# Fourteen picked tiles for twelve, and another order of the stages, in two layers of a graph attention kernel

## The chip, the cores and the metric

The kernel runs on one NeuronCore of a Trainium2 chip. The time is that of one launch on the device, in microseconds. TensorE (PE), VectorE (DVE), ScalarE (ACT) and GpSimd (POOL) each run their own list of instructions in order and wait for one another by semaphores; SyncE (SP) issues most DMAs.

## The reference

A graph with 6250 nodes of 64 features and 206250 directed edges, sorted by destination, goes through three layers of attention over the edges. Cut to what is computed:

```python
for i in range(3):
    q, k, v = (x @ W[i] + b[i] for W, b in ((Wq, bq), (Wk, bk), (Wv, bv)))
    e = edge_attr @ We[i]
    alpha = sum(q[dst] * (k[src] + e), -1) / sqrt(64)
    p = exp(alpha - segment_max(alpha, dst)[dst])
    w = p / segment_sum(p, dst)[dst]
    x = segment_sum((v[src] + e) * w[:, None], dst) + x @ Ws[i] + bs[i]
    x = relu(x)                  # and a layer norm after layers 0 and 1
out = layernorm(x_in + log_softmax(x))
```

## The kernel before

The edges are cut into tiles of 128. Six tiles make a chunk, four chunks a unit; there are 67 full units and one of four tiles. The destinations of a chunk lie within 32 nodes, so the four chunks of a unit share the 128 partitions of a score matrix, 32 each. The keys and values are not made for each edge: the weights are folded into the query, and an edge brings only the 64 features of its source node and its own 64 attributes. In layer 0 the kernel also sorts each unit's edges, so that in layers 1 and 2 the source nodes of a tile's two halves fall into known windows of 1024 nodes each. The change is about layers 1 and 2.

There are two ways to bring the source rows of a tile. POOL *gathers* it: one indirect DMA from the node table in DRAM (`gather`, L607; a small copy on ACT, the gate of L639, releases it). Or TensorE *picks* it: the table also lies in SBUF as two summands (`parts`), VectorE writes a one-hot matrix by comparing the tile's keys with a ramp (`hot`, L1342), and eight matmuls of 128x256 (L1404) serve one tile position of a pair of chunks, two tiles; VectorE then takes the right quarter of the result with a copy (L1365) and three predicated copies (L1367), called the evacuation, and ACT swaps some halves (L1353 to L1355). `PICKS` says how many of a unit's 24 tiles are picked, `depth` spreads them over the two pairs of chunks: 12 are (3, 3) positions. `Picker.picks` makes of this picks of one or two positions, here four a unit: of 16, 8, 16 and 8 matmuls. `Picker.aim` issues the `hot` instructions; at a unit's end it does so for the whole next unit. Four `hot` buffers and two banks of `ps_x` serve them.

The main loop goes over units; unit u has four quarters j, one for each chunk, and in the same pass it works on older and newer units:

- `turn(j)` (L1705, L1708): three transposes of chunk j's source rows into a bank `ps_a`, and two copies on ACT into `featT`, or `fourth` for the last chunk. The edges' half of it comes from DRAM by SP (`across`, L1685).
- `products(u-1, h)`, h = 0, 1 (L1718): half of the scores, into `ps_s` and `ps_p`; `most(u-1, h)` (L1732, L1745): mask and running maximum on VectorE; `powers(u-1)` (L1751): the exponential on ACT; `weights(u-1, h)` (L1765, L1768): the transposes of the exponentials through `ps_s` and `ps_p`, copied by ACT to `probT`.
- `sums(u-2)` (L1777): 48 matmuls in the profile, which add up the rows weighted by `probT` in `ps_p`; ACT copies them to `part`, SP stores that. `refill(u-2)` then gives the unit's buffer to unit u+2, and `free(u, j)` releases gathers for that unit.
- one pick for unit u+1 in each quarter, and one step of `finish` in quarter 0: every 5 to 6 units a group of four 128-node blocks is normalised (L1532, L1554) and, in layers 0 and 1, projected for the next layer (L1449, L1454, L1463).

Nothing reorders this: the instructions stand on each engine as the Python code issues them. A stage of an older unit is put between those of the present one so that no engine waits for another.

Of the kernel before, what the change touches and what calls it, by code (L numbers as in the profile page):

```python
# [19 lines left out]
P = 128  # L20
# [25 lines left out]
HALF = NW // 2  # L46
GC = 16
ROWS = 8
PICKS = ((8,), (12,), (12,))
LEAD = (3, 1, 1)  # L50
NH = WB // KB

# [377 lines left out]
def main_path(  # L430
# [1175 lines left out]
    class Unit:  # L1606
# [160 lines left out]
                self.probT = work.tile([P, TC, P], F32, name="probT", bufs=1)  # L1767
            nc.scalar.copy(self.probT[:, t0 : t0 + m, :n], p_t[:, :, :n])  # L1768

        def sums(self):  # L1770

            p_g = ps("g")[:, :P]
            batch = loaded[self.layer, self.k]
            for t in range(self.tiles):
                for j in range(self.m):
                    rows = slice(j * W, (j + 1) * W)
                    nc.tensor.matmul(  # L1777
                        p_g[rows, :].rearrange("n (h d) -> n h d", h=2),
                        self.probT[:, t, rows],
                        batch[:, j, t],  # L1780
                        start=(t == 0),
                        stop=(t == self.tiles - 1),
                    )
            nc.scalar.copy(self.part[: self.rows, :P], p_g[: self.rows, :])

        def store(self, half=None):
            for j in range(self.m):
# [81 lines left out]
    class Line:  # L1869


        def __init__(self, layer):
            self.layer = layer
            self.todo = list(zip(done, groups))
            self.stored = self.summed = 0
            self.halved = -1

        def sums(self, u):
            if u < 0:
                return  # L1880
            chunks[self.layer, u].sums()
            self.summed = u + 1

        def refill(self, u):
            if u >= 0:
# [54 lines left out]
    for layer in range(L):  # L1940
        line = Line(layer)
        assert not picked(layer, 0)

        def free(u, j):
            lead = 2 * LB if not layer else min(2 * LB, LB + u)
            release(layer, u * LB + j + (0 if not layer else 1) + lead, nc.scalar.copy)

        picker = Picker(layer)
        for u in range(NU - 2):
            this = chunks[layer, u]  # L1950
            picking = picker.batch(u + 1)
            n = len(picker.picks(u + 1))
            pace = 0 if layer else 6 if u < 3 else 3
            while not opened:
                move(1)
            line.sums(u - 2)
            line.products(u - 1, 0)
            if waiting:
                active.append(waiting.pop(0))
            for j in range(LB):  # L1960
                picker.quarter = j
                if j == 2 and not layer:
                    line.weights(u - 1, 0)
                this.turn(j)
                if j == 0:
                    line.refill(u - 2)
                free(u, j)
                if j == 0 and layer:
                    line.most(u - 1, 0)
                if j == 1 and layer:  # L1970
                    line.products(u - 1, 1)
                if j == 2 and layer:
                    line.powers(u - 1)
                if j == 3 and layer:
                    line.weights(u - 1, 1)
                if j == 1:
                    line.begun()
                    if not layer and placed(0, u + 1):
                        line.most(u - 1, 1)
                        line.powers(u - 1)  # L1980
                a, b = -(-n * j // LB), -(-n * (j + 1) // LB)
                if layer:
                    for i in range(max(b - a, 1)):
                        next(picking, None)
                        if not i and j == 1:
                            line.most(u - 1, 1)
                if j == 0:
                    close_up()
                else:
                    step()  # L1990
                if not layer:
                    move(pace - pace // 2)
                    if j == 0:
                        line.most(u - 1, 0)
                    for _ in range(b - a):
                        next(picking, None)
                    move(pace // 2)
                    picker.evacuate()
                if j == 0:
                    if not layer:  # L2000
                        line.products(u - 1, 1)
                        if not placed(0, u + 1):
                            line.most(u - 1, 1)
                            line.powers(u - 1)
                    ask(layer, u + 1)
                    if not placed(layer, u + 1):
                        chunks[layer, u + 1].across()
                if j == 2:
                    line.weights(u - 1, 0 if layer else 1)
                    if not this.placed:  # L2010
                        this.uncode()
                    decode(layer, u + 2)
                    if placed(layer, u + 1):
                        chunks[layer, u + 1].across()
                        chunks[layer, u + 1].shade()
                if j == 3:
                    line.store()
            assert next(picking, None) is None
            if any(not pair for _, pair, *_ in picker.swaps):
                picker.flush()  # L2020
            picker.ready.update(keys)
            picker.aim()
            for k in range(u + 2, u + 4):
                decode(layer, k)

        picker.flush()
        more = layer + 1 < L
        for _ in sorting:
            pass
        serve()  # L2030
        assert not picker.todo and not picker.hots
        if more:
            current[0] = layer
            lacking.extend(range(NW))
            if not layer:
                early.close()
                psum.append(ctx.enter_context(tc.tile_pool(name="psum", bufs=1, space=bass.MemoryType.PSUM)))
                bank_of.update({"g": "p", "node": "a", "s1": "p", "w0": "s"})
                stock[0] = ctx.enter_context(tc.tile_pool(name="picks", bufs=2))
                parts.append(stock[0].tile([P, 2, HALF * WB, D], F32R, name="parts", bufs=1))  # L2040
        u = NU - 2
        full = chunks[layer, u]
        line.sums(u - 2)
        line.refill(u - 2)
        line.scores(u - 1, 0)
        full.turn(0)
        free(u, 0)
        line.scores(u - 1, 1)
        ask(layer, u + 1)
        last = chunks[layer, u + 1]  # L2050
        last.across()
        last.shade()
        close_up()
        full.turn(1)
        free(u, 1)
        line.store()
        line.weights(u - 1, 0)
        close_up()
        full.turn(2)
        free(u, 2)  # L2060
        line.weights(u - 1, 1)
        full.turn(3)
        free(u, 3)
        free(u, 4)
        assert not pending
        close_up()
        line.scores(u, 0)
        line.scores(u, 1)
        line.sums(u - 1)
        line.refill(u - 1)  # L2070
        line.store()
        close_up()
        last.turn(0)
        last.uncode()
        line.weights(u, 0)
        line.weights(u, 1)
        close_up()
        line.scores(u + 1, 0)
        line.scores(u + 1, 1)
        line.sums(u)  # L2080
        line.refill(u)
        line.store()
        close_up()
        line.weights(u + 1, 0)
        line.weights(u + 1, 1)
        close_up()
        line.sums(u + 1)
        line.refill(u + 1)
        line.store()
        close_up()  # L2090
        if more:
            decode(layer + 1, 0)
            decode(layer + 1, 1)
            decode(layer + 1, 2)
            ask(layer + 1, 0)
            chunks[layer + 1, 0].across()
            chunks[layer + 1, 0].shade()
        while active or len(ending) > 1:
            close_up()
        while ending and (not more or (layer, groups[-1][0]) not in written):  # L2100
            close_up()
        if more:
            assert all((layer, g) in written for g, n in groups)
            for k in range(FB):
                if (layer + 1, k) not in loaded:
                    fetch(layer + 1, k)
                if k:
                    await_turn(layer + 1, k)
                else:
                    gather_all(layer + 1, k)  # L2110
            while lacking or held:
                reload(layer + 1)
            while ending:
                close_up()
# [45 lines left out]
```

## Time and profile before

| | |
|---|---|
| median of 3 runs | 4164.22 us (4156.0 to 4164.31) |
| profiled execution: time, span of its profile | 4160.32 us, 4158.5 us |
| TensorE's mean granted clock | 0.925 |
| PE, PEld (weight loads) busy | 3390.2 us (82%), 2406.9 us (58%) |
| DVE, ACT, POOL busy | 3094.5 us (74%), 2344.7 us (56%), 2819.2 us (68%) |
| gathers on POOL in layers 1 and 2 (L607) | 1592 of 985 ns |

A group's line names line, engine, operation, result and operands; then the count, the busy time in us, the mean ns of one, the idle time ahead of it and what ended that. In a timeline a row has start and length in us, and in brackets the idle time ahead of it with its releaser. A run of matmuls is pipelined, so the next run may start before it ends. Layer 0 takes the first 1900 us or so of the span, layers 1 and 2 some 1100 each.

### The profile page before, as it was taken

How to read it: one execution, taken by the hardware profiler on the slowest of the kernel's cores; microseconds unless marked ns; L12 is line 12 of the kernel's file. 1: busy time of each engine (PE TensorE's matmuls, PEld its weight loads, DVE VectorE, ACT ScalarE, POOL GpSimd, SP SyncE). 2: the span in 40 equal slices, each digit the busy share in tenths (PEclk: the TensorE clock that was granted, in tenths of full speed). 3: DMA queues.
4: the chain of work that ended last, by engine and by line, in shares of the span. 5: the costliest groups of instructions: out<-in, count | busy, mean ns of one | idle time of the engine just before them, and what ended most of it. 6: DMA issues, size and time to landing. Idle time of an engine off the chain costs nothing.

```text
span 4158.5 us, 105258 instructions
## 1 busy us (share of the span) xinstructions
PE 3390.2 (82%) x34183; PEld 2406.9 (58%) x34183; DVE 3094.5 (74%) x10306; ACT 2344.7 (56%) x5994; POOL 2819.2 (68%) x2774
## 2 busy tenths in 40 slices
PE   3779988998999899995778788888758788787776
PEld 2345555555555555553666666666646666666664
DVE  5678888888888888874566677677646767777775
ACT  1345555555565565563555556665535666666665
POOL 5466666666666666663777777777747777777774
PEclk9889999999999999996899999999969999999997
DMA  5657676667667767675677777777657677777774
GB/s 120 165 163 194 175 186 177 168 181 185 174 176 186 181 174 187 171 199 137 151 181 185 189 191 188 185 190 197 167 129 183 176 185 186 185 185 190 185 185 100
DMA packets 787997, 728.88 MB, mean 175 GB/s; under 512 B 487336, under 2 KB 612450, under 8 KB 787440
## 3 DMA queue, kind: packets, MB, share of 16 engines
q1 hardware_dynamic: 630436, 504.14, 47.5%
q0 software_dynamic: 88448, 90.75, 11.8%
q10 hardware_dynamic: 68556, 127.16, 8.6%
q8 instruction: 278, 4.55, 0.5%
q14 instruction: 279, 2.29, 0.2%
HBM read 562.78 MB, written 158.81 MB: 174 GB/s over the span
## 4 chain that ended last, share of the span: by engine, by line


## 5 line engine op out<-in xcount | busy, mean ns | idle before, releaser
L607 POOL DMA_INDIRECT feat<-x,gate x1592 | 1568.8, 985 | 485.3 <-issue 367.3
L607 POOL DMA_INDIRECT feat<-in_x,gate x1100 | 1177.7, 1071 | 676.0 <-ACT gate L639 360.8
L1404 PE MATMUL ps_x<-parts,hot 128*128 128x256 f32 x6336 | 942.5, 301 | 0.0
L1404 PEld LDWEIGHTS ps_x<-parts,hot 128*128 128x128 f32 x6336 | 842.2, 202 | 82.2 <-DVE feat L1367 65.6
L1708 ACT COPY featT<-ps_a 64x384 f32<-64x384 f32 x1320 | 626.7, 475 | 410.3 <-PE ps_a L1705 392.7
L1367 DVE COPY_PREDICATED feat<-which,ps_x 128x256 f32<-128x256 int32 (+1 forms) x1584 | 592.8, 374 | 54.3
L1365 DVE COPY feat<-ps_x 128x256 f32<-128x256 f32 (+1 forms) x528 | 187.8, 356 | 580.8 <-PE ps_x L1404 564.9
L1705 PE MATMUL ps_a<-ident,feat 128*128 128x128 f32 x2380 | 450.2, 290 | 145.2 <-DMA feat<-x,gate 107.0
L1705 PEld LDWEIGHTS ps_a<-ident,feat 128*128 128x128 f32 x2380 | 285.1, 145 | 354.1 <-issue 261.1
L1081 DVE TENSOR_SCALAR hit<-ruler,pos 128x384 bf16<-128x384 f16 x1608 | 457.3, 326 | 7.3 <-PE ps_m L1101 6.6
L1342 DVE TENSOR_SCALAR hot<-keys,rank 128x512 fp32r<-128x512 f16 (+1 forms) x1040 | 432.7, 483 | 5.4 <-DMA keys<-keyS 5.4
L1777 PE MATMUL ps_p<-feat,probT 128*32 128x128 f32 x6600 | 242.8, 300 | 84.6 <-ACT probT L1768 73.8
L1092 PE MATMUL ps_x<-hit,raw 128*64 128x384 bf16 x1608 | 296.0, 364 | 0.5 <-DVE hit L1081 0.4
L1092 PE MATMUL ps_x<-hit,rest 128*64 128x384 bf16 x1608 | 277.8, 342 | 0.0
L1092 PE MATMUL ps_x<-hit,end 128*64 128x384 bf16 x1608 | 277.3, 341 | 0.0
L1777 PEld LDWEIGHTS ps_p<-feat,probT 128*32 128x32 f32 x6600 | 198.9, 122 | 123.2 <-ACT probT L1768 98.2
L1718 PE MATMUL ps_s<-featT,q 128*32 128x384 f32 x1866 | 235.2, 509 | 32.6 <-DVE most L1732 25.4
L1765 PE MATMUL ps_s<-ident,prob 128*128 128x128 f32 (+1 forms) x417 | 83.4, 313 | 215.4 <-ACT prob L1751 214.3
L1751 ACT ACTIVATE prob<-prob,part 128x768 f32<-128x768 f32 x204 | 190.0, 932 | 83.8 <-DVE part L1745 75.5
L1125 ACT COPY eT<-ps_x 128x384 f32<-128x384 f32 x268 | 129.3, 483 | 122.5 <-PE ps_x L1092 89.6
L1765 PEld LDWEIGHTS ps_s<-ident,prob 128*128 128x128 f32 (+1 forms) x417 | 47.8, 152 | 245.9 <-ACT prob L1751 241.5
L1143 ACT COPY feat<-ps_a 128x384 f32<-128x384 f32 x256 | 122.1, 481 | 120.6 <-PE ps_a L1135 89.7
(280 smaller groups left out, 6019.1 us busy)
## 6 DMA issues: line engine op xcount, KB each, us to landing
featT<-eaS SPq DMA_DIRECT2D x658, 192.0 KB
feat<-eaP SPq DMA_DIRECT2D x134, 768.0 KB
raw<-in_ea SPq DMA_DIRECT2D x536, 96.0 KB
eaS<-eT ACTq DMA_DIRECT2D x134, 384.0 KB
keys<-keyS SPq DMA_DIRECT2D x132, 384.0 KB
eaP<-feat ACTq DMA_DIRECT2D x128, 384.0 KB
shade<-maskS SPq DMA_DIRECT2D x198, 192.0 KB
fourth<-eaS SPq DMA_DIRECT2D x134, 192.0 KB
```

The costliest lines, as they stand in the source:

```text
L607: nc.gpsimd.indirect_dma_start(out=feat[:, c, t, 0], out_offset=None, in_=xts[layer][:, :], in_offset=bass.IndirectOffsetOnAxis(ap=index[: ...
L1081: nc.vector.tensor_scalar(hit, ruler, self.pos[:, at : at + 1], None, ALU.is_equal)
L1092: nc.tensor.matmul(self.px[j * D : (j + 1) * D, :HE], self.parts[2 * h + i].thirds[part][:, j, t * D : (t + 1) * D], self.hits[h, 2 * i + ...
L1342: nc.vector.tensor_scalar(hot[:, h], keys[self.layer, k][:, first : first + n], rank[:, h : h + 1], None, ALU.is_equal)
L1365: nc.vector.tensor_copy(found, px[:, :, :, 0])
L1367: nc.vector.copy_predicated(found, which[:, :, :, b].bitcast(I32).unsqueeze(3).to_broadcast([P, 2, m, D]), px[:, :, :, b],)
L1404: nc.tensor.matmul(px[:, t - t0, v].rearrange("p b d -> p (b d)"), hot[:, h, (2 * pair + v) * P : (2 * pair + v + 1) * P], those[:, i, b0 ...
L1705: nc.tensor.transpose(pt[:, t * P : (t + 1) * P], rows[:, 2 * t * D : 2 * (t + 1) * D], ident)
L1708: nc.scalar.copy(featT[:, :, h, :], pt[h * D : (h + 1) * D, : n * P].rearrange("d (i e) -> d i e", e=P))
L1718: nc.tensor.matmul(p_s[rows, :w], self.q[:, rows], self.featT[j][:, cols], start=True, stop=True)
L1751: nc.scalar.activation(self.prob[:n, : self.cols], self.prob[:n, : self.cols], AF.Exp, bias=neg, accum_out=self.part[:n, P + 1 : P + 2],)
L1777: nc.tensor.matmul(p_g[rows, :].rearrange("n (h d) -> n h d", h=2), self.probT[:, t, rows], batch[:, j, t], start=(t == 0), stop=(t == sel ...
```

## The change

`PICKS` goes from 12 to 14 in layers 1 and 2. `depth` gives (4, 3) positions, so the four picks are of 16, 16, 16 and 8 matmuls, all four `hot` buffers are in use (the fourth half as wide), and ten tiles are gathered instead of twelve. And the quarters of layers 1 and 2 get a new order: weights of unit u-2 in quarter 0, its sums in 1, both products and the first maximum of u-1 in 2 around the pick, the second maximum and the exponential in 3 ahead of the pick. The weights of a unit thus come one pass later than before. The core of the diff:

```diff
-PICKS = ((8,), (12,), (12,))
+PICKS = ((8,), (14,), (14,))
...
             while not opened:
                 move(1)
-            line.sums(u - 2)
-            line.products(u - 1, 0)
+            if not layer:
+                line.sums(u - 2)
+                line.products(u - 1, 0)
...
                 this.turn(j)
-                if j == 0:
-                    line.refill(u - 2)
-                free(u, j)
-                if j == 0 and layer:
-                    line.most(u - 1, 0)
-                if j == 1 and layer:
-                    line.products(u - 1, 1)
-                if j == 2 and layer:
-                    line.powers(u - 1)
-                if j == 3 and layer:
-                    line.weights(u - 1, 1)
-                if j == 1:
-                    line.begun()
-                    if not layer and placed(0, u + 1):
+                if layer:
+                    if j == 2:
+                        line.products(u - 1, 0)
+                        line.most(u - 1, 0)
+                        line.begun()
+                    if j == 3:
                         line.most(u - 1, 1)
                         line.powers(u - 1)
+                        free(u, j)
+                else:
...
                 if layer:
-                    for i in range(max(b - a, 1)):
+                    for _ in range(max(b - a, 1)):
                         next(picking, None)
-                        if not i and j == 1:
-                            line.most(u - 1, 1)
+                    if j == 0:
+                        line.weights(u - 2, 0)
+                        line.weights(u - 2, 1)
+                    if j == 1:
+                        line.sums(u - 2)
+                        line.refill(u - 2)
+                        free(u, j)
+                    if j == 2:
+                        line.products(u - 1, 1)
+                        free(u, j)
...
-                if j == 2:
-                    line.weights(u - 1, 0 if layer else 1)
+                if j == 2 and not layer:
+                    line.weights(u - 1, 1)
...
                 if j == 3:
                     line.store()
+                    if layer:
+                        decode(layer, u + 2)
+                        chunks[layer, u + 1].across()
+                        chunks[layer, u + 1].shade()
...
         full = chunks[layer, u]
+        if layer:
+            line.weights(u - 2, 0)
+            line.weights(u - 2, 1)
```

The `else` branch keeps the old order for layer 0. `sums` can now be issued in parts, but each call still issues all of it.

TensorE in the middle of layer 1, before, from the first weights of a unit to the first pick of the next; `hot_` and a number is one `hot` tile, and an instruction of fp32 that the profile counts twice stands here once:

```order
L1765 MATMUL ps_s<-ident,prob 128x128 x3
L1705 MATMUL ps_a<-ident,feat 128x128 x3
L1765 MATMUL ps_p<-ident,prob 128x128 x3
L1404 MATMUL ps_x<-parts,hot_38625 128x256 x8
L1777 MATMUL ps_p<-feat,probT 32x128 x24
L1718 MATMUL ps_s<-featT,q 32x384 x3
L1718 MATMUL ps_s<-fourth,q 32x384
L1705 MATMUL ps_a<-ident,feat 128x128 x3
L1404 MATMUL ps_x<-parts,hot_38852 128x256 x8
L1404 MATMUL ps_x<-parts,hot_38855 128x256 x8
```

The same engine after, from the last transposes of a unit to the sums in the next:

```order
L1705 MATMUL ps_a<-ident,feat 128x128 x3
L1404 MATMUL ps_x<-parts,hot_38837 128x256 x8
L1705 MATMUL ps_a<-ident,feat 128x128 x3
L1404 MATMUL ps_x<-parts,hot_39073 128x256 x8
L1404 MATMUL ps_x<-parts,hot_39076 128x256 x8
L1765 MATMUL ps_s<-ident,prob 128x128 x3
L1765 MATMUL ps_p<-ident,prob 128x128 x3
L1705 MATMUL ps_a<-ident,feat 128x128 x3
L1404 MATMUL ps_x<-parts,hot_39079 128x256 x8
L1404 MATMUL ps_x<-parts,hot_39082 128x256 x8
L1779 MATMUL ps_p<-feat,probT 32x128 x24
```

Between a unit's last pick and the first of the next stood the sums, a product and a transpose; now only the transpose does, and the weights and sums stand behind the first and the second pick.

VectorE before, from the second maximum of a unit to its last evacuation and the `hot` tiles of the next unit:

```order
L1732 ISA prob,most<-ps_p,shade,most 128x384
L1732 ISA most 128x1
L1745 TENSOR_SCALAR part<-most 128x1
L1365 COPY feat<-ps_x 128x2x128
L1367 COPY_PREDICATED feat<-which,ps_x 128x2x128 x3
L1365 COPY feat<-ps_x 128x2x64
L1367 COPY_PREDICATED feat<-which,ps_x 128x2x64 x3
L1331 TENSOR_TENSOR which<-kbs,four 128x64
L1342 TENSOR_SCALAR hot_39795<-keys,rank 128x512 x2
L1342 TENSOR_SCALAR hot_39798<-keys,rank 128x512 x2
L1342 TENSOR_SCALAR hot_39801<-keys,rank 128x512 x2
```

VectorE after, the same stretch:

```order
L1365 COPY feat<-ps_x 128x2x128
L1367 COPY_PREDICATED feat<-which,ps_x 128x2x128 x3
L1732 ISA prob,most<-ps_p,shade,most 128x384
L1732 ISA most 128x1
L1745 TENSOR_SCALAR part<-most 128x1
L1365 COPY feat<-ps_x 128x2x64
L1367 COPY_PREDICATED feat<-which,ps_x 128x2x64 x3
L1331 TENSOR_TENSOR which<-kbs,four 128x64
L1342 TENSOR_SCALAR hot_40052<-keys,rank 128x512 x2
L1342 TENSOR_SCALAR hot_40055<-keys,rank 128x512 x2
L1342 TENSOR_SCALAR hot_40058<-keys,rank 128x512 x2
L1342 TENSOR_SCALAR hot_40061<-keys,rank 128x256 x2
```

The second maximum now stands between the evacuations of picks 2 and 3, and the `hot` tiles still follow the last evacuation, with a fourth one of half the width.

More of the change, by code (lines that the diff above doesn't have):

```diff
@@ L1768, in weights, with sums @@
             nc.scalar.copy(self.probT[:, t0 : t0 + m, :n], p_t[:, :, :n])
-        def sums(self):
-            p_g = ps("g")[:, :P]
+        def sums(self, first, upto):
+            if not first:
+                self.summed = ps("g")[:, :P]
+            p_g = self.summed
             batch = loaded[self.layer, self.k]
-            for t in range(self.tiles):
+            for t in range(first, upto):
                 for j in range(self.m):
@@ L1783, in sums @@
                     )
-            nc.scalar.copy(self.part[: self.rows, :P], p_g[: self.rows, :])
+            if upto == self.tiles:
+                nc.scalar.copy(self.part[: self.rows, :P], p_g[: self.rows, :])
         def store(self, half=None):
@@ L1874, in __init__, with sums @@
             self.todo = list(zip(done, groups))
-            self.stored = self.summed = 0
+            self.stored = self.summed = self.tile = 0
             self.halved = -1
-        def sums(self, u):
-            if u < 0:
+        def sums(self, u, upto=TC):
+            if u < self.summed:
                 return
-            chunks[self.layer, u].sums()
-            self.summed = u + 1
+            this = chunks[self.layer, u]
+            upto = min(upto, this.tiles)
+            if upto > self.tile:
+                this.sums(self.tile, upto)
+                self.tile = upto
+            if upto == this.tiles:
+                self.summed = u + 1
+                self.tile = 0
         def refill(self, u):
@@ L1964, in main_path @@
                 this.turn(j)
-                if j == 0:
-                    line.refill(u - 2)
-                free(u, j)
-                if j == 0 and layer:
-                    line.most(u - 1, 0)
-                if j == 1 and layer:
-                    line.products(u - 1, 1)
-                if j == 2 and layer:
-                    line.powers(u - 1)
-                if j == 3 and layer:
-                    line.weights(u - 1, 1)
-                if j == 1:
-                    line.begun()
-                    if not layer and placed(0, u + 1):
+                if layer:
[4 more added lines that the diff above has]
+                    if j == 3:
                         line.most(u - 1, 1)
                         line.powers(u - 1)
+                        free(u, j)
[4 more added lines that the diff above has]
+                    if j == 1:
+                        line.begun()
+                        if placed(0, u + 1):
+                            line.most(u - 1, 1)
+                            line.powers(u - 1)
                 a, b = -(-n * j // LB), -(-n * (j + 1) // LB)
                 if layer:
-                    for i in range(max(b - a, 1)):
+                    for _ in range(max(b - a, 1)):
                         next(picking, None)
-                        if not i and j == 1:
-                            line.most(u - 1, 1)
+                    if j == 0:
+                        line.weights(u - 2, 0)
+                        line.weights(u - 2, 1)
+                    if j == 1:
+                        line.sums(u - 2)
+                        line.refill(u - 2)
+                        free(u, j)
+                    if j == 2:
+                        line.products(u - 1, 1)
+                        free(u, j)
                 if j == 0:
```

## The prediction

> **What bounds the kernel now.** I read the windows of the two layers first, then the groups of instructions in layer 1, then the timelines of GpSimd, TensorE and VectorE in single units.
>
> The windows, one for the middle of layer 1 and one for that of layer 2. After the length stand the busy microseconds (and instructions) of PE, PEld, DVE, ACT and POOL, then the granted clock, the DMA share and GB/s:
>
> ```profile
> 2100.00:3000.00 900.00, 729.33 (x7776) 596.58 (x7773) 635.78 (x1956) 538.40 (x1390) 687.82 (x697) 0.96 0.74 186
> 3150.00:4050.00 900.00, 721.96 (x7642) 607.25 (x7643) 632.30 (x1975) 554.01 (x1406) 686.95 (x700) 0.92 0.73 185
> ```
>
> PE has the most busy time, but POOL sets the pace. The group of its gathers in layer 1, and two places of its timeline:
>
> ```profile
> L607 POOL DMA_INDIRECT feat<-x,gate x697 | 688.8, 988 | 212.5 <-issue 160.7 <-DMA feat<-x,gate 15.9 <-DVE hot L1342 7.9
> ...
> 2511.44 0.94 POOL L607 DMA_INDIRECT feat<-x,gate  x1 [0.30 <-issue]
> ...
> 2515.18 1.25 POOL L607 DMA_INDIRECT feat<-x,gate  x1 [0.30 <-DMA feat<-x,gate]
> ```
>
> 688.8 busy and 212.5 idle make 901: the idle time is only the 0.30 ahead of every gather, so POOL issues gathers without a pause. A gather costs 0.94 + 0.30 = 1.24 us, and about 0.3 more beside VectorE's `hot` instructions. A unit has twelve. Layer 1 thus takes 12 x 900/697 = 15.49 us a unit, layer 2 12 x 900/700 = 15.43. The others wait for POOL, as TensorE does at 2632.20 (1.43 us for a gather) in one undisturbed unit:
>
> ```profile
> 2626.16 2.14 PE L1404 MATMUL ps_x<-parts,hot 128*128 128x256 f32 x16
> 2628.14 0.49 PE L1705 MATMUL ps_a<-ident,feat 128*128 128x128 f32 x3
> 2628.56 0.52 PE L1718 MATMUL ps_p<-featT,q 128*32 128x384 f32 x3
> ...
> 2629.34 1.21 PE L1404 MATMUL ps_x<-parts,hot 128*128 128x256 f32 x8
> 2630.39 0.38 PE L1705 MATMUL ps_a<-ident,feat 128*128 128x128 f32 x2
> 2632.20 0.33 PE L1705 MATMUL ps_a<-ident,feat 128*128 128x128 f32 x1 [1.43 <-DMA feat<-x,gate]
> 2632.30 2.12 PE L1404 MATMUL ps_x<-parts,hot 128*128 128x256 f32 x16
> 2634.61 0.55 PE L1765 MATMUL ps_s<-ident,prob 128*128 128x128 f32 x3 [0.18 <-ACT prob L1751]
> 2634.99 0.49 PE L1705 MATMUL ps_a<-ident,feat 128*128 128x128 f32 x3
> 2635.32 0.49 PE L1765 MATMUL ps_p<-ident,prob 128*128 128x128 f32 x3
> 2635.56 1.20 PE L1404 MATMUL ps_x<-parts,hot 128*128 128x256 f32 x8
> 2637.81 1.52 PE L1777 MATMUL ps_p<-feat,probT 128*32 128x128 f32 x48 [1.05 <-ACT probT L1768]
> 2639.14 0.50 PE L1718 MATMUL ps_s<-featT,q 128*32 128x384 f32 x3
> ...
> 2639.90 0.55 PE L1705 MATMUL ps_a<-ident,feat 128*128 128x128 f32 x3
> 2640.20 2.13 PE L1404 MATMUL ps_x<-parts,hot 128*128 128x256 f32 x16
> ```
>
> **The change part by part.** *Two gathers fewer.* POOL needs 10 x 1.24 us and some 0.28 more for three gathers beside the longer `hot` run: 13.2 us. It no longer sets the pace if anything else needs more. The gathers are also released later (the refill now stands behind the sums of quarter 1), but they are those of unit u+2, more than a unit ahead of their use: no cost.
>
> *Eight matmuls more.* The second pick of a unit grows from 8 to 16. A run of 16 holds TensorE for 1.98 us (2626.16 to 2628.14), one of 8 for 1.05 (2629.34 to 2630.39): +0.93 us.
>
> *The new order.* What can bind now is a ring through two engines. VectorE builds the one-hot tiles of the next unit only behind the last evacuation of this one, as before; but TensorE then had the sums, a product and a transpose (2637.81 to 2640.20) between pick 3 and the next pick 0. Now it has one transpose. So the ring is: pick 0, both weights, transpose, pick 1, sums, transpose, first product, pick 2, and from there VectorE: evacuation of pick 2, second maximum, evacuation of pick 3, `which`, first `hot`, then pick 0. VectorE's rows:
>
> ```profile
> 2618.64 0.61 DVE L1732 CUSTOM_DVE_ANT_0 prob<-ps_p,shade,most 128x384 f32<-128x384 f32 x1
> ...
> 2619.36 0.41 DVE L1365 COPY feat<-ps_x 128x256 f32<-128x256 f32 x1
> 2619.81 1.41 DVE L1367 COPY_PREDICATED feat<-which,ps_x 128x256 f32<-128x256 int32 x3
> 2622.76 0.29 DVE L1365 COPY feat<-ps_x 128x128 f32<-128x128 f32 x1 [1.53 <-PE ps_x L1404]
> ...
> 2623.96 0.22 DVE L1331 TENSOR_TENSOR which<-kbs,four 128x64 f32<-128x64 uint8 x1
> 2624.09 2.46 DVE L1342 TENSOR_SCALAR hot<-keys,rank 128x512 fp32r<-128x512 f16 x6
> ...
> 2634.46 0.42 DVE L1365 COPY feat<-ps_x 128x256 f32<-128x256 f32 x1 [1.87 <-PE ps_x L1404]
> ```
>
> TensorE's part, from start to start: pick 0 1.98; weights, weights, transpose 1.00 (by the steps 0.38, 0.33 and 0.30 at 2634.61, 2634.99 and 2639.90); pick 1 1.98; sums 1.33; transpose 0.42; product 0.78 (2628.56 to 2629.34); pick 2 to its evacuation 2.16 (2632.30 to 2634.46): 9.65 us. VectorE's part: 1.76 (1.86 less the 0.10 by which a waiting instruction starts early, as between 2622.76 and 2624.09), 0.72, 1.20, 0.13, and a third of 2.46, 0.82: 4.63. With 0.05 to hand over, the ring is **14.33 us**. The chain is serial; I allow 0.2 either way.
>
> What lies beside it at no cost: the evacuations of picks 0 and 1 and the first maximum run on VectorE while TensorE is at work, with some 1.5 us to spare; the transposes' copies, the gate copies and the swaps on ScalarE have over a microsecond each. Two waits of TensorE go: the one for the exponential (0.18 in this unit; the weights now come a quarter later) and the 1.05 us for `probT` (now covered by transpose and pick 1, 2.28 us). On SP the loads of `featT` and `shade` move from quarter 2 to 3 and stand there behind the second product and the second maximum; queued behind them are the next `q` loads and the refill, all needed a unit later: no cost; if that cover went, ScalarE's first copy of the next unit would wait, at most for those loads.
>
> Other work on TensorE in the ring: the node groups that are finished meanwhile, in the same 900 us of layer 1:
>
> ```profile
> L1454 PE MATMUL ps_a<-xT,eq 64*128 64x512 f32 x19 | 10.8, 644 | 0.0
> L1554 PE MATMUL ps_a<-ve,wT 128*128 128x64 f32 x80 | 10.5, 274 | 0.0
> L1463 PE MATMUL ps_a<-ws,xT 64*128 64x65 f32 x72 | 9.9, 278 | 0.0
> L1532 PE MATMUL ps_a<-ident,w 128*128 128x128 f32 x40 | 6.2, 278 | 0.0
> L1449 PE MATMUL ps_a<-ident,y 128*64 128x128 f32 x40 | 6.0, 272 | 0.0
> ```
>
> 43.4 us in 58.1 units is 0.75 us each; of every run some 0.16 overlaps the next one (1.21 against 1.05 above), so about **0.61**. Layer 2 has L1532 and L1554 alone: 16.7 us, by the same steps **0.23**.
>
> *The clock.* In the ring TensorE ends its last transpose at 7.49 + 1.98 + 0.76 + 0.30 + 1.05 + 0.49 = 12.07 us after pick 0 and then has nothing until 14.33: a stretch of **2.26 us** in each unit. The granted clock changes on a grid of 3.41 us. Two neighbouring pairs of such windows:
>
> ```profile
> 3956.60:3960.01 3.41, 1.57 (x14) 1.38 (x13) 3.16 (x10) 1.81 (x5) 2.50 (x4) 1.00 0.93 204
> 3960.01:3963.42 3.41, 3.41 (x33) 3.11 (x35) 0.74 (x3) 2.35 (x6) 2.80 (x3) 0.50 0.83 218
> ...
> 2058.79:2062.20 3.41, 1.59 (x12) 1.42 (x12) 0.63 (x3) 1.70 (x5) 2.50 (x4) 1.00 0.81 228
> 2062.20:2065.61 3.41, 3.01 (x64) 2.39 (x65) 3.31 (x10) 0.95 (x3) 2.79 (x3) 1.00 0.32 52
> ```
>
> After 1.57 us of work in a window the next runs at half clock, after 1.59 it doesn't: about 1.84 us of idleness in one window is enough. A stretch of 2.26 us gives that in (3.41 - 2.26) + 2 x (2.26 - 1.84) = 1.99 of 3.41 us of phase, 0.58 of the units if the phase were random. It is not quite: a unit at full clock moves the grid by 14.33 - 13.65 = +0.68 us, a slowed one by 15.76 - 17.07 = -1.31, which balances at 0.34. I take the middle, 0.46. What a slowed window costs:
>
> ```profile
> 2605.24 0.90 PE L1765 MATMUL ps_s<-ident,prob 128*128 128x128 f32 x3 [3.05 <-ACT prob L1751]
> ...
> 2607.07 1.75 PE L1404 MATMUL ps_x<-parts,hot 128*128 128x256 f32 x8
> ```
>
> From the first weights to pick 3 it took 1.83 us against 0.95 (2634.61 to 2635.56), the pick 1.75 against 1.20: 1.43 us lost, now on the ring. 0.46 x 1.43 = **0.66 us** a unit. The Trainium skill ("TensorE: Matmul & The Clock Gate", on the clock gate and its oscillation) says that the array falls to half clock after an idle window of about 3.4 us and advises no gaps above that. By that rule a gap of 2.26 us would cost nothing, which is the first rival below; the two pairs of windows speak against it.
>
> *Sum.* Layer 1: 14.33 + 0.61 + 0.66 = 15.60 against 15.49, +0.11 x 65 units = +7 us. Layer 2: 14.33 + 0.23 + 0.66 = 15.22 against 15.43, -14 us. At each layer's end the weights of one more unit are left over: about 1 us and the 1.05 us wait, +4 for both. Layer 0 keeps its order and its eight picks. Together -3 us on the profiled execution's 4160.3: **4157 us**. That execution lies 4 us under the median of the runs shown (4164.2), within what they scatter. About 0.2%, 8 us, is what a measurement can tell from no change.
>
> **The rivals.** *The clock stays up.* If the stretch is under 1.84 us, or the gate asks for more idleness, the 0.66 goes: 14.94 and 14.56 us a unit, -36 - 57 + 4: 4071 us. For it: the gap of 1.43 us at 2632.20 has no slow run behind it. Against it: the ring's stretch is 0.4 us over the limit that the windows show.
>
> *The clock falls after nearly every stretch*, the case on the other side. Then 1.43 us a unit are lost: 16.37 and 15.99, +57 + 36 + 4: 4257 us. It decides from a share of 0.52 on, where the sum is 8 us above the time before. For it: layer 2 runs at a clock of 0.92 even now, and every further wait in the ring, which I can't see in this trace, lengthens the stretch or the ring just so.
>
> *POOL stays the bound*, with TensorE and VectorE running ahead: 13.2 us a unit, 4160 - 65 x (2.29 + 2.23) = 3866 us. It needs the `hot` tiles built earlier, which the new order doesn't do.
>
> **How the numbers follow.** The forecast's case has a chance of 0.50 (ring 0.2 us off: 26 us; share 0.34 to 0.58: 22 us; together 4109 to 4205): faster 0.20, same 0.10, slower 0.20. Clock up 0.18, POOL 0.02, clock down or an unseen wait in the ring 0.30. Faster 0.40, same 0.10, slower 0.50. The range 4070 to 4255 leaves out POOL, half of the clock-up case and a quarter of the clock-down case, 0.19.
>
> **What would show it.** Gathers with idle time far above 0.30; a `hot` run as the releaser of TensorE's pick 0 and one stretch of about 2.3 us ahead of it in each unit; no wait of the sums for `probT`; half-clock windows right behind about half of the stretches. It is wrong if POOL still issues without a pause, if TensorE's long wait stands elsewhere, or if units differ from 15.6 and 15.2 us by over 0.5.

## The result and the profile after

The changed kernel takes 4202.1 us (median of 4 runs, 4200.9 to 4213.8) against 4160.1 us before: a ratio of 1.0107 [1.009, 1.0123], 1.1% slower. Forecast were 4157 us, no change. The profiled execution took 4213.8 us with a span of 4212.0; it is the slowest of the four, 53 us above the one shown of before.

The windows of the two layers, as before with the busy time of PE, PEld, DVE, ACT and POOL, then granted clock, DMA share and GB/s:

```profile
2100.00:3000.00 900.00, 790.59 (x7843) 654.18 (x7844) 677.99 (x1992) 520.39 (x1332) 550.02 (x555) 0.93 0.68 179
3150.00:4050.00 900.00, 787.05 (x8037) 658.84 (x8036) 695.70 (x2059) 557.73 (x1409) 586.54 (x589) 0.94 0.71 183
```

POOL fell from 688 to 550 and 587 busy microseconds and is no longer the bound. The group of its gathers in layer 1 now has 350 us of idle time, where it had 212:

```profile
L607 POOL DMA_INDIRECT feat<-x,gate x555 | 550.8, 992 | 350.3 <-ACT gate L639 211.9 <-issue 101.8 <-DVE hot L1342 16.7
```

POOL now waits for the release of a gather on ACT (L639). ACT itself waits mostly for TensorE: its three longest waits in layer 1 are for results in `ps_s` (111.8 us), `ps_p` (97.7) and `ps_a` (89.4). What TensorE waits for, in the same two stretches (total us, times, longest):

```profile
PE ps_x L1404 <- DVE hot L1342: 109.2, 56, 2.0
...
PE ps_x L1404 <- DVE hot L1342: 109.9, 57, 2.1
```

There is one wait a unit, 1.95 us in the mean, for the first `hot` tile. No gather and no load appears as a cost: the later refill and the moved loads on SP are hidden, as forecast. One unit on TensorE, from the transposes ahead of pick 0 to the next pick 0 and its weights:

```profile
2619.05 1.20 PE L1404 MATMUL ps_x<-parts,hot 128*128 128x256 f32 x8
2620.08 0.49 PE L1705 MATMUL ps_a<-ident,feat 128*128 128x128 f32 x3
2622.49 2.36 PE L1404 MATMUL ps_x<-parts,hot 128*128 128x256 f32 x16 [1.92 <-DVE hot L1342]
2624.70 0.49 PE L1765 MATMUL ps_s<-ident,prob 128*128 128x128 f32 x3
2625.02 0.49 PE L1765 MATMUL ps_p<-ident,prob 128*128 128x128 f32 x3
2625.35 1.00 PE L1554 MATMUL ps_a<-ve,wT 128*128 128x64 f32 x8
2626.19 0.50 PE L1705 MATMUL ps_a<-ident,feat 128*128 128x128 f32 x3
2626.44 2.15 PE L1404 MATMUL ps_x<-parts,hot 128*128 128x256 f32 x16
2628.53 1.52 PE L1779 MATMUL ps_p<-feat,probT 128*32 128x128 f32 x48
2629.97 0.55 PE L1705 MATMUL ps_a<-ident,feat 128*128 128x128 f32 x3
...
2637.86 2.96 PE L1404 MATMUL ps_x<-parts,hot 128*128 128x256 f32 x16 [1.93 <-DVE hot L1342]
2640.62 0.84 PE L1765 MATMUL ps_s<-ident,prob 128*128 128x128 f32 x3
```

The sums (L1779) no longer wait for `probT`. From pick 0 to pick 0 it is 15.37 us, and 14.53 without the node-group work of 2625.35 (0.84). The second pick 0 ran into half clock: 2.96 us for 2.36. VectorE in the stretch ahead of the first pick 0:

```profile
2618.06 0.42 DVE L1365 COPY feat<-ps_x 128x256 f32<-128x256 f32 x1 [1.32 <-PE ps_x L1404]
2618.52 1.41 DVE L1367 COPY_PREDICATED feat<-which,ps_x 128x256 f32<-128x256 int32 x3
2619.82 0.61 DVE L1732 CUSTOM_DVE_ANT_0 prob<-ps_p,shade,most 128x384 f32<-128x384 f32 x1
...
2620.54 0.28 DVE L1365 COPY feat<-ps_x 128x128 f32<-128x128 f32 x1
...
2621.73 0.22 DVE L1331 TENSOR_TENSOR which<-kbs,four 128x64 f32<-128x64 uint8 x1
2621.87 3.11 DVE L1342 TENSOR_SCALAR hot<-keys,rank 128x512 fp32r<-128x512 f16 x8
```

This is the forecast ring link by link: evacuation of pick 2, second maximum, evacuation of pick 3, `which`, `hot`, and pick 0 at 2622.49. Two pairs of neighbouring clock windows from this stretch:

```profile
2601.76:2605.17 3.41, 1.43 (x11) 1.04 (x10) 3.27 (x12) 2.93 (x8) 2.50 (x4) 1.00 0.42 98
2605.17:2608.59 3.42, 3.42 (x19) 3.42 (x18) 2.34 (x7) 0.57 (x3) 2.81 (x3) 0.50 1.03 205
2618.83:2622.24 3.41, 1.74 (x14) 1.50 (x14) 3.20 (x12) 2.50 (x6) 2.50 (x4) 1.00 0.30 58
2622.24:2625.65 3.41, 3.15 (x26) 3.02 (x26) 3.38 (x10) 1.99 (x7) 2.69 (x3) 1.00 1.03 233
```

The window in which the stretch lies whole (1.43 us of work) is followed by one at half clock; the one in which it lies in part (1.74) isn't.

To compare the kernels I take the mean spacing of the `which` rows (L1331), one for each unit, in the middle of each layer (some 700 to 900 us from 2063 and from 3172 us on), and count the half-clock windows from 2063 to 2960 and from 3172 to 3890 (time below full clock over 3.41 us):

| kernel | layer 1: us/unit, half-clock windows | layer 2 | wait of pick 0 for `hot`, layer 1 |
|---|---|---|---|
| before | 15.54, 20 | 15.58, 34 | |
| after | 16.25, 38 | 15.60, 26 | 1.95 |
| e1, new order, twelve picks | 15.60, 31 | 15.53, 25 | 1.69 |
| e2, old order, fourteen picks | 15.86, 8 | 15.64, 12 | |
| e4, six matmuls in the stretch | 15.22, 0 | 14.72, 0 | 0.51 |
| e9, two | 15.27, 3 | 14.72, 0 | 1.41 |
| e5, one | 16.30, 38 | 15.42, 21 | 1.64 |
| e6, three elsewhere | 17.06, 39 | 16.55, 33 | 1.95 |
| e7, six elsewhere | 17.31, 26 | 17.22, 31 | 1.95 |
| e8, `hot` and keys earlier | 14.24 | 13.89 | 0.75 |

Layer 1 lost 0.71 us x 65 units = 46 us and layer 2 about 1 us; that is 47 of the 53 us between the two profiled executions.

### The profile page after: what moved, and what is told of

It is laid out like the page before. It is cut to its first block, busy times and chain, and to the rows that moved or that the text cites. A ratio compares the mean times of both kernels' runs of the same rounds, so it can differ in the third digit from the quotient of the medians.

```text
span 4212.0 us, 106939 instructions
## 1 busy us (share of the span) xinstructions
PE 3583.5 (85%) x35239; PEld 2570.5 (61%) x35239; DVE 3251.7 (77%) x10570; ACT 2355.4 (56%) x5994; POOL 2571.2 (61%) x2510
## 4 chain that ended last, share of the span: by engine, by line
## 5 line engine op out<-in xcount | busy, mean ns | idle before, releaser
L607 POOL DMA_INDIRECT feat<-x,gate x1328 | 1318.0, 992 | 751.1 <-ACT gate L639 411.0
L1404 PE MATMUL ps_x<-parts,hot 128*128 128x256 f32 x7392 | 1117.4, 305 | 247.3 <-DVE hot L1342 245.3
L1404 PEld LDWEIGHTS ps_x<-parts,hot 128*128 128x128 f32 x7392 | 995.4, 204 | 373.1 <-issue 333.9
L1367 DVE COPY_PREDICATED feat<-which,ps_x 128x256 f32<-128x256 int32 (+1 forms) x1584 | 650.3, 411 | 54.4
L1342 DVE TENSOR_SCALAR hot<-keys,rank 128x512 fp32r<-128x512 f16 (+1 forms) x1304 | 512.0, 460 | 4.5 <-DMA keys<-keyS 4.5
L1705 PE MATMUL ps_a<-ident,feat 128*128 128x128 f32 x2380 | 429.4, 289 | 36.9 <-DMA feat<-x,src_b 31.2
L1708 ACT COPY fourth<-ps_a 64x384 f32<-64x384 f32 x268 | 127.1, 474 | 216.7 <-PE ps_a L1705 214.9
L1779 PE MATMUL ps_p<-feat,probT 128*32 128x128 f32 x6600 | 219.3, 280 | 15.4 <-DVE most L1732 10.0
L1732 DVE CUSTOM_DVE_ANT_0 prob<-ps_s,shade 128x384 f32<-128x384 f32 x204 | 113.5, 557 | 127.6 <-ACT featT L1708 64.8
L1779 PEld LDWEIGHTS ps_p<-feat,probT 128*32 128x32 f32 x6600 | 179.2, 112 | 39.8 <-DVE most L1732 13.9
L1768 ACT COPY probT<-ps_s 128x384 f32<-128x384 f32 (+1 forms) x139 | 65.9, 474 | 237.5 <-PE ps_s L1765 237.3
```

The source lines that it names most:

```text
L607: nc.gpsimd.indirect_dma_start(out=feat[:, c, t, 0], out_offset=None, in_=xts[layer][:, :], in_offset=bass.IndirectOffsetOnAxis(ap=index[: ...
L1342: nc.vector.tensor_scalar(hot[:, h], keys[self.layer, k][:, first : first + n], rank[:, h : h + 1], None, ALU.is_equal)
L1367: nc.vector.copy_predicated(found, which[:, :, :, b].bitcast(I32).unsqueeze(3).to_broadcast([P, 2, m, D]), px[:, :, :, b],)
L1404: nc.tensor.matmul(px[:, t - t0, v].rearrange("p b d -> p (b d)"), hot[:, h, (2 * pair + v) * P : (2 * pair + v + 1) * P], those[:, i, b0 ...
L1705: nc.tensor.transpose(pt[:, t * P : (t + 1) * P], rows[:, 2 * t * D : 2 * (t + 1) * D], ident)
L1708: nc.scalar.copy(featT[:, :, h, :], pt[h * D : (h + 1) * D, : n * P].rearrange("d (i e) -> d i e", e=P))
```

## The experiments

**e1: the new order with twelve picks.** The changed kernel with the old number of picks:

```diff
-PICKS = ((8,), (14,), (14,))
+PICKS = ((8,), (12,), (12,))
```

> The new order with 12 picks. Ring theory (a serial ring through TensorE and VectorE sets the pace, lengthened by half-clock windows): the second pick has 8 matmuls again, so the ring falls from 14.45 by 0.93 to 13.5 us a unit, under the 15.45 of twelve gathers; POOL sets the pace again: 4160 us, 10 either way. Load theory (TensorE is simply full, 88% busy, and the eight matmuls are the price): 4160 too. Gate theory (the gathers are released too late in the new order, POOL waits up to 5.6 us for a gate): POOL, again the bound, loses its waits: 4200 us or more.

Measured: 4159.8 us, 0.9997 [0.9983, 1.0011]. POOL's gathers in layer 1 (2100 to 3000 us):

```profile
L607 POOL DMA_INDIRECT feat<-x,gate x695 | 689.0, 991 | 211.9 <-issue 152.7 <-DMA feat<-x,gate 15.6 <-DVE hot L1342 9.1
```

As many gathers as before and no pause: POOL is the bound again, and the order alone changes nothing that can be measured. That speaks against the gate theory, which expected 4200 us or more. The half-clock windows, 31 and 25 of them, cost nothing that can be measured here, since POOL sets the pace.

**e2: fourteen picks in the old order.** The kernel before with

```diff
-PICKS = ((8,), (12,), (12,))
+PICKS = ((8,), (14,), (14,))
```

> 14 picks in the old order. Ring theory: the sums, a product and a transpose cover VectorE's evacuation and hot tiles again, so the ring is TensorE's own 13 us or so and its waits for the exponential and for probT, 1 us or more each: about 15 us a unit, 4100 to 4160 us. Load theory: the same work, so 4200 us as with the new order.

Measured: 4172.8 us, 1.003 [1.0016, 1.0043], 13 us above the upper end that the ring theory gave and 27 below the load theory's 4200. TensorE's waits in layer 1:

```profile
PE ps_s L1765 <- ACT prob L1751: 94.7, 55, 2.5
PE ps_p L1777 <- ACT probT L1768: 63.5, 54, 1.2
```

In the old order the ring goes through the exponential (1.72 us a unit) and `probT` (1.18), part of which POOL's pace had covered before. A unit without node-group work and without half clock takes 14.84 us in layer 1 (median of 12), so by these units the new order shortens the ring by about 0.35 us. But the old one splits TensorE's idleness in two and has only 8 and 12 half-clock windows where the changed kernel has 38 and 26. In layer 1 the order gains on the ring and loses more on the clock; in layer 2 the two about cancel (15.60 for 15.64).

**e3: the `hot` tiles one evacuation earlier.** The changed kernel, in quarter 3 of layers 1 and 2, lets the first three of the next unit's `hot` tiles be built ahead of the evacuation of pick 3:

```diff
                         free(u, j)
+                        picker.ready.update(keys)
```

> All of the change, but the first three hot tiles of the next unit stand on VectorE ahead of the last evacuation. Ring theory: the ring loses evacuation 3 and drops from 14.45 to about 13.1 us, level with POOL's 13.2; the idle stretch falls from 2 us to under 1, so hardly a half-clock window is left: some 13.8 and 13.5 us a unit against 16.23 and 15.62, about 3930 us, 40 either way. Load theory and gate theory: no change from 4200, 10 either way.

Measured: 3999.9 us, 0.9611 [0.9588, 0.9634]. The direction was right, but the time is 30 us above the range's end. The load and gate theories, which expected no change, are out. The undisturbed unit fell from 14.45 to 13.4 us: the ring through VectorE is confirmed as what binds. The rest went to a new wait; one row of what VectorE waits for from 3150 to 3900 us:

```profile
DVE hot L1342 <- DMA keys<-keyS: 26.9, 19, 3.3
```

In layer 2 SP issued the load of the keys only some 6 us ahead of their new use (median 6.2 us, 4.6 to 9.3), behind the stores of the parts.

**e4: the stretch filled.** The changed kernel with six matmuls of the identity with itself, into the bank that pick 0 then overwrites (their results are not used):

```diff
                 px = ps(bank)...
+                if self.layer and not pair and not t0:
+                    for _ in range(6):
+                        nc.tensor.matmul(px[:, 0, 0]...[:, :P], ident, ident, start=True, stop=True)
```

> All of the change, and six matmuls without use (identity by identity, into the bank that pick 0 overwrites) in TensorE's idle stretch. Ring theory: the ring stays, but no window is idle enough for half clock: 0.67 and 0.57 windows a unit at 1.6 us less, 15.2 and 14.7 us a unit, about 4075 us, 25 either way, and a granted clock near 1.0 in both layers. Load theory: TensorE gets fuller by 0.9 us a unit: 4200 to 4320 us. Gate theory: 4200.

Measured: 4077.6 us, 0.9806 [0.978, 0.9831]. On TensorE they stand in the stretch (first row), and pick 0 still waits for VectorE (second):

```profile
2628.24 1.50 PE L1399 MATMUL ps_x<-ident 128*128 128x128 f32 x12
2630.25 2.47 PE L1409 MATMUL ps_x<-parts,hot 128*128 128x256 f32 x16 [0.51 <-DVE hot L1342]
```

Nothing on the ring is shorter, and 124 us go, with all of the half-clock windows: that is what they cost. By this run a unit without them takes 15.22 and 14.72 us, against 14.94 and 14.56 in the prediction's first rival.

**e5: one matmul in the stretch** (`range(1)`).

> The changed kernel with one identity matmul (0.25 us, result unused) ahead of each unit's pick 0 in layers 1 and 2, where e4 had six. The stretch ahead of pick 0 is 1.92 to 1.98 us in the trace of the changed kernel; one matmul leaves about 1.7. Threshold theory (a window of 3.41 us with over about 1.84 us of idleness brings the next one to half clock, and nothing else does): nearly all half-clock windows go and the time is that of six matmuls, 4065 to 4090. Rival, load theory (the clock follows the mean load of TensorE): a sixth of the 124 us that six brought, about 4180. Rival, the stretch as the gate sees it is longer than the trace's idle time by 0.15 or more: partly or wholly unchanged, 4140 to 4202.

Measured: 4180.0 us, 1.0059 [1.0039, 1.0079]. The threshold as I had it doesn't hold for this stretch. The wait that was left, in the two layers (2100 to 3000 and 3150 to 4050 us):

```profile
PE ps_x L1409 <- DVE hot L1342: 90.0, 55, 1.7
...
PE ps_x L1409 <- DVE hot L1342: 94.9, 58, 1.8
```

With 1.64 us of idleness layer 1 has as many half-clock windows as with 1.95. Four pairs of windows:

```profile
2886.80:2890.21 3.41, 1.70 (x12) 1.31 (x11) 3.27 (x12) 2.91 (x8) 2.50 (x4) 1.00 0.34 52
2890.21:2893.63 3.42, 3.42 (x18) 3.27 (x16) 2.43 (x8) 0.70 (x2) 2.70 (x3) 0.50 1.01 232
2347.49:2350.91 3.42, 1.83 (x13) 1.63 (x14) 3.35 (x10) 2.88 (x8) 2.73 (x3) 1.00 0.90 199
2350.91:2354.32 3.41, 3.41 (x17) 3.08 (x16) 2.48 (x7) 1.58 (x3) 2.57 (x3) 0.50 0.98 284
2903.87:2907.28 3.41, 1.82 (x16) 1.62 (x14) 3.21 (x12) 3.02 (x4) 2.58 (x3) 1.00 0.25 40
2907.28:2910.69 3.41, 3.35 (x26) 3.15 (x27) 3.38 (x9) 2.90 (x10) 2.55 (x3) 1.00 0.98 222
2610.32:2613.73 3.41, 1.80 (x16) 1.60 (x15) 3.24 (x12) 2.79 (x7) 2.74 (x3) 1.00 0.39 90
2613.73:2617.15 3.42, 3.39 (x28) 3.19 (x29) 3.35 (x10) 2.01 (x6) 2.51 (x4) 1.00 1.03 223
```

A window with 1.70 us of work, and even one with 1.83, is followed by half clock, while others with 1.80 and 1.82 are not: about 1.8 here, not 1.57, and not sharp in this measure. Nor is it a limit on PE's busy time that holds for every kernel of this case. Of the full-clock windows with 1.60 to 1.84 us of work, in the same stretches of both layers, 54 of 63 are followed by half clock in e5, but only 3 of 10 in the changed kernel, none of 16 in e2 and none of 22 in the kernel before. A pair of e2:

```profile
3759.64:3763.05 3.41, 1.76 (x15) 1.56 (x14) 3.22 (x9) 3.22 (x9) 1.87 (x2) 1.00 0.36 63
3763.05:3766.47 3.42, 2.21 (x25) 2.01 (x28) 1.75 (x8) 3.01 (x8) 2.51 (x4) 1.00 0.53 122
```

The load theory's value, 4180, came out, so it needed another run.

**e9: two matmuls** (`range(2)`), which sets the two theories apart.

> The changed kernel with two identity matmuls (0.5 us, results unused) ahead of each unit's pick 0 in layers 1 and 2. With one (e5) pick 0 still waited 1.64 us (90.0 us in 55 waits), and 39 and 28 half-clock windows were left in the two layers' middles, all behind windows with up to 1.83 us of work. So the limit is not 1.57 us of work in 3.41, as I had it, but about 1.8. Threshold theory with the new limit: two matmuls leave a wait of about 1.4, each window keeps about 2.0 us of work, and nearly all half-clock windows go: 4065 to 4095, about what six brought. Rival, load theory (the clock follows the mean load): a third of the 124 us of six, about 4160.

Measured: 4079.2 us, 0.9815 [0.9799, 0.9832]: one matmul brings 22 us, two bring 123, six 124. In this stretch that is a threshold and no mean load. TensorE's wait in layer 1 (2100 to 2950 us), and the windows of both layers:

```profile
PE ps_x L1409 <- DVE hot L1342: 79.1, 56, 1.4
```

```profile
2100.00:2950.00 850.00, 768.59 (x8106) 630.93 (x8100) 677.75 (x2002) 519.57 (x1337) 556.91 (x557) 1.00 0.72 191
3150.00:4000.00 850.00, 766.96 (x8326) 636.86 (x8325) 700.44 (x2107) 560.25 (x1417) 579.79 (x583) 1.00 0.75 196
```

At 1.41 us of idleness a unit the clock stays at 1.00, at 1.64 it falls nearly as often as at 1.95. For this stretch, with such matmuls in it, the limit lies between the first two.

**e6 and e7: three and six matmuls where TensorE is busy,** ahead of pick 1:

```diff
+                if self.layer and not pair and t0:
+                    for _ in range(3):      # e7: 6
```

> The changed kernel with three identity matmuls (0.75 us, results unused) ahead of pick 1 of each unit's picks, where TensorE has work anyway, so that the stretch ahead of pick 0 stays. Grid theory: I carried the grid of 3.413 us windows through 65 units of 12.5 us of work and 1.95 us of idleness, with the next window at 0.53 of the speed where a window holds under 1.58 us of work. For the changed kernel that gives 16.2 us a unit in layer 1 and 15.6 in layer 2 (measured 16.23 and 15.62). With 0.75 us more work it gives 16.95 and 16.85, close to five windows (17.07): 4202 + 65 x (0.72 + 1.23) = 4329, and 4315 to 4350. Rival, a random phase: the share of slowed units stays as it is, and each unit is 0.75 longer: 4202 + 130 x 0.75 = 4300. Rival, load theory: more load keeps the clock up, under 4202.

> As the run with three, with six identity matmuls (1.5 us) ahead of pick 1. Grid theory: 17.1 us a unit in both layers, five windows, with only 0.3 of the units slowed in layer 1 and 0.55 in layer 2: 4202 + 65 x (0.87 + 1.45) = 4353, so only some 20 us above the run with three (within 40). Random phase: 4202 + 130 x 1.5 = 4397, 97 above the run with three.

Measured: 4308.4 us, 1.038 [1.0352, 1.0407], and 4363.3 us, 1.0506 [1.0483, 1.053]. The same six matmuls that save 124 us in the stretch cost 161 here, so load as such doesn't hold the clock up. The run with three came 7 us below the range that the grid gave, nearer to the additive 4300, and alone tells nothing apart. The step from three to six is 55 us, not 97, with 26 half-clock windows for 39 in layer 1: part of the added work is given back by the grid, as expected, though more remains than the 24 us worked out. The run with six is 10 us above the grid's 4353 and 34 below the additive 4397. By units, the grid gave 16.95 and 16.85 us for three matmuls and 17.1 in both layers for six; the table has 17.06 and 16.55, 17.31 and 17.22. So the two runs bear the grid out in part only.

**e8: the keys earlier as well.** e3, with the next load of the keys a quarter earlier on SP, ahead of the store:

```diff
                         line.products(u - 1, 1)
                         free(u, j)
+                        decode(layer, u + 3)
...
-            picker.ready.update(keys)
+            picker.ready.update(x for x in keys if x[1] <= u + 2 or x[0] > layer)
```

> The kernel of e3 (hot tiles built one evacuation earlier) with the load of the keys issued a quarter earlier on SP, ahead of the store of the parts. In e3 SP issued them only 6.6 us before VectorE wanted them, and VectorE waited for them 26.9 us in 750 us of layer 2 and 8 us in layer 1, each such wait leaving TensorE a long stretch with a half-clock window behind it. My theory: these waits go, and with them a part of the half-clock windows: 3950, 3920 to 3985. Rival, the load itself is late (the DMA engines are 78 percent busy): no change from 4000.

Measured: 3956.4 us, 0.952 [0.9493, 0.9547], the fastest of all. The wait for the keys (3150 to 3900 us), and the windows of the two layers:

```profile
DVE hot L1342 <- DMA keys<-keyS: 6.5, 9, 1.3
```

```profile
2100.00:2900.00 800.00, 748.95 (x7988) 610.66 (x7987) 678.45 (x2023) 521.81 (x1352) 564.31 (x567) 1.00 0.79 205
3150.00:3900.00 750.00, 699.60 (x7600) 576.53 (x7594) 653.17 (x1992) 525.42 (x1330) 541.54 (x546) 0.99 0.80 205
```

26.9 us of that wait became 6.5, pick 0 waits 0.75 us for `hot`, and the clock stays up without a filling. The DMA engines are busier than in e3 (0.80 in layer 2 for 0.76), so the late load came from SP's order and not from busy DMA engines.

## Why the prediction was wrong

**What binds: right.** POOL's pauses, the one stretch ahead of pick 0, its releaser, the missing wait for `probT`, the half-clock windows behind the stretches, the hidden loads: each is in the trace, and e3 and e8 moved the time by moving that ring. Only the unit of layer 1, 16.25 us for 15.6, was off by more than the 0.5 us that the prediction allowed.

**The ring, 14.33: 14.45 to 14.53.** VectorE's part was 4.43 us (2618.06 to 2622.49) for 4.68 (4.63 and the 0.05 to hand over). TensorE's was longer: pick 0 took 2.21 for 1.98 (2622.49 to 2624.70), since its third matmul waits for the second instruction of the `hot` run, which ends at 2622.87, pick 1 took 2.09 (2626.44 to 2628.53) for 1.98 and the sums 1.44 (2628.53 to 2629.97) for 1.33. The stretch was therefore 1.95 us and not 2.26. Node-group work: 0.72 and 0.22 (e4 less 14.5) for 0.61 and 0.23.

**The share of slowed units, 0.46: the step that failed.** It was 38 of 55 units in layer 1 (0.69) and 26 of 46 in layer 2 (0.57). The forecast was the middle of a random phase (0.58) and a balance (0.34), and it is the balance that was off: it used 14.33 us for the unit in both layers, without the node-group work. With the prediction's own 14.94 and 14.56 us it would have been 0.65 and 0.46 and the middles 0.61 and 0.52, at and above the 0.52 from which the change was said to cost time. The sizes that the later runs gave move it further. In layer 1 an undisturbed unit of 15.22 moves the grid by +1.57, a slowed one of 16.71 by -0.36, balanced at 0.81. In layer 2, 14.72 and 16.28 move it by +1.07 and -0.79, balanced at 0.58. With the balance alone put at these values the middles are 0.70 and 0.58, close to what was measured.

The random phase kept its size by luck. The stretch was 1.95 us for 2.26, which with the limit of 1.84 makes (1.46 + 0.22)/3.41 = 0.49; a limit of 1.6, as e5 and e9 give it for their stretch, makes (1.46 + 0.70)/3.41 = 0.63. That limit of 1.84 rested on two windows, and which limit holds for the changed kernel is open. All of this is worked out after the fact with what the later runs gave. Whether the middle of the two is the right formula was not tested by itself.

**The loss for each slowed unit, 1.43:** 1.49 and 1.56 (16.25 - 15.22 over 0.69, 15.60 - 14.72 over 0.57). Share and loss together make 1.03 and 0.88 us a unit where 0.66 was forecast.

**The base of layer 2, 15.43: 15.58.** I divided by twelve gathers a unit; at 900/700 us a gather 15.58 us are 12.1. In layer 1 it was 15.54 for 15.49.

**The sum:** layer 1 came out at 16.25 for 15.60, layer 2 at 15.60 for 15.22. So layer 1 changed by +0.71 for +0.11, layer 2 by +0.02 for -0.21: 65 x (0.60 + 0.23) = 54 us, about the 56 between the forecast change of -3 us and the profiled +53. Of the 0.60 in layer 1, 0.37 are the clock and 0.28 the ring with the node-group work, less 0.05 for the base.

**The rivals.** POOL as the bound is out: in layer 1 it has 350.3 us of idle time ahead of 555 gathers, where gathers without a pause would have 0.30 us each, 167. What took over is the mechanism of the case on the other side, at two thirds of its price: it was said to decide from a share of 0.52, and both layers were above that. The case of a clock that stays up was worked out as 4071; with the clock held up by filling, the kernel takes 4077.6 and 4079.2. That it is so close is in part luck: units of 15.22 and 14.72 us for 14.94 and 14.56 make 29 us more, and units of before that were 0.05 and 0.15 us longer than I had give 13 of them back. The rule cited there from the Trainium skill ("TensorE: Matmul & The Clock Gate", section "HAM oscillation — how this bites in real kernels": no idle gaps above about 3.4 us) is not enough here: gaps of 1.95 us in the changed kernel, and of 1.64 us in e5, were followed by half clock in more than half of the units of layer 1.

**What stays open:** what the gate counts. PE's busy time in the profile orders the windows only roughly (1.70 and 1.83 fell, 1.80 and 1.82 didn't), and windows with 1.60 to 1.84 us were nearly always followed by half clock in e5 and never in e2.

## What to carry to other kernels

When work is taken off the bounding engine, look at how the next ring arranges TensorE's idleness. In e2 two separate waits, 1.72 and 1.18 us in the mean of layer 1, left 8 and 12 half-clock windows; here one stretch of 1.6 to 2 us in each unit brought 21 to 38, and cost 1.5 us of every unit that it slowed. Several waits are no safety by themselves: the kernel before, whose wait for the exponential was up to 3.1 and 3.8 us long in the two layers, had 20 and 34. To price such a stretch, use the whole length of a unit, since its distance from a multiple of 3.41 us enters the balance that failed here, and take the limit from many windows and not from two. The cure that cost least was 0.5 us of useless matmuls in the stretch (-123 us), the better one a one-hot tile built one step earlier with its load issued in time (-246 us).

## What the hardware showed that I had not expected

In this stretch the clock responds by a step: 1.95, 1.64, 1.41 and 0.51 us of waiting a unit gave 38, 38, 3 and 0 half-clock windows in layer 1. Yet the same busy time of PE in a window doesn't bring the same clock in every kernel, as e5 and e2 show. And slower units can lock onto the grid: in layer 1 of the changed kernel half-clock windows follow each other at 17.07 us, five windows of 3.41, for several units in a row (from 2226 to 2294 us, for instance). This agrees with the balance, by which the layer with more work on TensorE is hit harder; no run changes that alone.
